# Building the scans' weights: 66 small transfers handed out between matmuls instead of in one block

## The chip, the cores and the metric

The kernel runs on one core of a Trainium2 chip. The metric is the device time of one launch in microseconds (us). TensorE (PE in the profile), VectorE (DVE), ScalarE (ACT), GpSimd (POOL) and SyncE (SP) each work through an instruction list of their own, strictly in order. They meet only through semaphores. SP and POOL also start transfers (DMA): a transfer stands in its engine's list like any other instruction, and what comes after it in the list waits until it has been issued.

## The reference: what is computed

The input x is 4 images of 96 channels and 128 x 128 pixels. Two layers follow, each added to its input. The first is a selective scan over the image in four directions:

```python
z = conv1x1(group_norm(x), in_w) + in_b             # 96 -> 192 channels
z = silu(depthwise3x3(z) + dw_b)
xs = [z row by row, z column by column, both reversed]       # 4 directions
dts, Bs, Cs = split(einsum(xs, x_proj_weight))      # 6 + 1 + 1 rows per direction
delta = softplus(einsum(dts, dt_projs_weight) + dt_projs_bias)
h[l] = exp(-exp(A_logs) * delta[l]) * h[l-1] + delta[l] * Bs[l] * xs[l]
y = sum over directions of (h * Cs + Ds * xs)
x = x + (layer_norm(y) * ln_w + ln_b) @ out_w + out_b
```

The second layer normalises x again, splits it by sign, convolves it several times (3 x 3), builds an attention between the channels whose result is used as the weights of one more 3 x 3 convolution, and mixes all of it into the output. This change concerns only the preparation of two weight tables for the scans of the first layer.

## The kernel before, in words

**Stages.** The kernel goes through: statistics of image 0; projection of image 0 (input convolution, 3 x 3 and silu in one set of matmuls); projections of images 1 to 3, with the scans woven between them; normalisations, direct maps and attention of the second layer, image by image. The first strips of image 0 are where the change lies.

**Projection (`project`).** Image 0 is worked in 16 strips of 8 rows. A strip has three groups of matmuls at L613, called q = 0, 1 and 2. The first two give channels 0 to 127 of four rows each, the third the remaining 64 channels of all eight rows. Each group fills a PSUM bank. ScalarE takes the tanh of it (L488), and VectorE multiplies it by the bank (L489); only then is the bank free. There are three such banks for everything in this stage (pool `psl`, bufs=3), given out in turn. Between q = 1 and q = 2 a small matmul (`rows_out`, L515) projects the strip before to the 48 rows that hold dts, B and C; after q = 2 twelve tiny transposing matmuls (`cols_out`, L556) follow. The input rows of the next strip are loaded by SP (L438, tile `y`), normalised by ScalarE (L456), and copied by SP into shifted positions (L464).

**Woven work.** `project` is a generator: it yields 11 times in a strip (three times in each group, and after `rows_out` and `cols_out`), so that other work can be put between. Beside the matmuls of image 0 run the statistics of images 1 and 2 (`image_stats`). Each step of them either issues a load of 96 x 512 values to a tile `xst` on POOL's list (L401) or takes `bn_stats` of such a tile on VectorE (L404). There are two tiles, so a load waits for the `bn_stats` of two loads ago. A strip holds four loads and four `bn_stats`.

**Weights of the scans (`other_weights`).** This generator makes `wdt` and `wbc`, two bf16 tables whose rows lie on the partitions in the order of the scan's input rows. It splits `dt_projs_weight` into three bf16 pieces (`split3`, ScalarE L207 and VectorE L209), then copies the pieces into place with transfers within the on-chip memory: for six row groups, three pieces, three places each, 54 transfers of 3 or 6 KB to `wdt` (L246), and for each of the six row groups two transfers of at most 0.8 KB to `wbc` (L249). All 66 are on POOL's list. After them come the output weights: VectorE scales `outw` by `lnw` (L251), TensorE makes two small products `pb` (L256) and `pw` (L263), and VectorE uses them (L259, L266).

**Order.** The top level steps these generators by hand. When two strips of image 0 are ready it takes the pair weights of the second layer (`made`, stored to `wd`), then the whole rest of `other_weights`, and only then goes on with the projection. The program is written out in this order, and every engine keeps it; from the projection of image 0 to the end of the scans, dependencies between neighbours make this explicit (`in_order`). The scans take `wdt` and `wbc` as the weights of their matmuls (L727) from the middle of image 0's projection on.

Of the kernel before, what the change touches and what calls it, by code (L numbers as in the profile page):

```python
# [62 lines left out]
def kernel(  # L63
# [138 lines left out]
    def split3(pool, src, shape):  # L202

        pieces = []
        for i in range(3):
            t = pool.tile(shape, BF16, name=f"piece{i}", tag=f"piece{i}")
            nc.scalar.copy(t, src)  # L207
            if i < 2:
                nc.vector.tensor_sub(src, src, t)  # L209
            pieces.append(t)  # L210
        return pieces

    def other_weights():

        wdt = const.tile([128, 3, NK, 128], BF16, name="wdt", tag="wdt")
        wbc = const.tile([128, 3, 2, 128], BF16, name="wbc", tag="wbc")
        outws = const.tile([C, 2, C], F32, name="outws", tag="outws")  # L220
        outbs = const.tile([C, 1], F32, name="outbs", tag="outbs")
        with (
            tc.tile_pool(name="w0", bufs=1, side="right") as w0,
            tc.tile_pool(name="ps0", bufs=1, space=PSUM, side="right") as ps0,
        ):
            wf = w0.tile([RANK, NK, 2 * C], F32, name="wf")
            nc.gpsimd.dma_start(wf, dt_wT)
            outw = w0.tile([C, 2, C], F32, name="outw")
            nc.sync.dma_start(outw, out_wT)
            one = w0.tile([3, 128], BF16, name="one")  # L230
            nc.vector.memset(one, 1.0)
            nc.vector.memset(wdt, 0.0)
            nc.vector.memset(wbc, 0.0)
            yield
            flat = "p k c -> p (k c)"
            pieces = split3(w0, wf.rearrange(flat), [RANK, NK * 2 * C])
            for row, ch, g, p, n in (
                (row, *part)
                for img, *part in PARTS
                for row in ((KI * img,) if part[1] == 1 else (0, 64))  # L240
            ):
                for w in range(3):
                    src = pieces[w].rearrange("p (k c) -> p k c", k=NK)[:, :, ch : ch + n]
                    for i in range(3):
                        at = row + w * 18 + i * RANK
                        nc.gpsimd.dma_start(wdt[at : at + RANK, g, :, p : p + n], src)  # L246
                for q in range(2):
                    at = row + 54 + q
                    nc.gpsimd.dma_start(wbc[at : at + 5 : 2, g, q, p : p + n], one[:, :n])  # L249
            for j in range(2):  # L250
                nc.vector.tensor_scalar(  # L251
                    outws[:, j], outw[:, j], lnw[:, j : j + 1], None, ALU.mult
                )
            pb = ps0.tile([C, 1], F32, name="pb")
            for j in range(2):
                nc.tensor.matmul(  # L256
                    pb, lhsT=outw[:, j], rhs=lnb[:, j : j + 1], start=(j == 0), stop=(j == 1)
                )
            nc.vector.tensor_add(outbs, pb, outb)  # L259

            pw = ps0.tile([C, C], F32, name="pw")
            for j in range(2):
                nc.tensor.matmul(  # L263
                    pw, lhsT=mean192, rhs=outws[:, j], start=(j == 0), stop=(j == 1)
                )
            nc.vector.tensor_sub(outws, outws, pw.unsqueeze(1).to_broadcast([C, 2, C]))  # L266
        yield wdt, wbc, outws, outbs
# [14 lines left out]
    def co_run(left, right, pace):  # L282


        owed = 0.0
        for cost in left:
            owed += cost * pace
            while owed > 0:
                got = next(right, 0)
                if got == 0:  # L290
                    return
                if got is None:
                    owed = 0.0
                    break
                owed -= got
# [20 lines left out]
    def traced():  # L316
        return nc.cur_bb.bb.instructions
# [21 lines left out]
    def drain(gen):  # L339
        for _ in gen:  # L340
            pass
# [48 lines left out]
    def image_stats(b, pool):  # L390

        stats = pool.tile([C, NCH, 6], F32, name="stats", tag="stats")
        mv = const.tile([C, 2], F32, name=f"stats{b}", tag=f"stats{b}")

        def run(p2, ahead, queue):
            xf = x[b].rearrange("c h w -> c (h w)")
            tiles = []
            for i in range(NCH + ahead - 1):
                if i < NCH:
                    tiles.append(p2.tile([C, CH], F32, name="xst", bufs=ahead))  # L400
                    queue.dma_start(tiles[-1], xf[:, bass.ts(i, CH)])  # L401
                yield 0.7
                if i >= ahead - 1:
                    nc.vector.bn_stats(stats[:, i - ahead + 1], tiles.pop(0))  # L404
                yield 0.7
            nc.vector.bn_aggr(mv, stats.rearrange("p c s -> p (c s)"))

        return mv, run
# [768 lines left out]
    def new_map(name):  # L1177

        m = dram.tile([C, (H + 2) * PW + 4], F32, name=name, tag=name, bufs=1)
        nc.sync.dma_start(m[:, 0:PW], zeros[:, 0:PW])  # L1180
        nc.sync.dma_start(m[:, (H + 1) * PW :], zeros[:, 0 : PW + 4])
        return m
# [13 lines left out]
    def pair_weights():  # L1196

        four, nine, taps = [], [], []  # L1200
        with tc.tile_pool(name="wq", bufs=2, side="right") as pw:
            for pair in ((aw1, aw3), (aw2, w_conv2)):
                g = pw.tile([C, 3, 3, 2, C], F32, name="g")
                for j, src in enumerate(pair):
                    v = src.rearrange("c (h w) o -> c h w o", w=3)
                    for w in range(3):

                        nc.sync.dma_start(g[:, :, w, j], v[:, :, w if j else 2 - w])
                taps.append(g)
            yield  # L1210
            for i, g in enumerate(taps):
                g = g.rearrange("p h w j o -> p h w (j o)")
                wt = pw.tile([C, 3, 4, 2 * C], F32, name="wt")
                s = pw.tile([C, 3, 2 * C], F32, name="s")
                products_weights(wt, g, s)
                for made, t in ((four, wt), (nine, g)):
                    wd = dram.tile(
                        list(t.shape), F32, name=f"wd{t.shape[2]}{i}", tag=f"wd{t.shape[2]}{i}", bufs=1
                    )
                    nc.sync.dma_start(wd, t)  # L1220
                    made.append(wd)
        yield four, nine
# [577 lines left out]
    def projections(images, weights, stats, wp, ps):  # L1800
        for b in images:
            beside = []
            for i in {0: range(1, NB - 1), 1: (NB - 1,)}.get(b, ()):
                stats[i], run = image_stats(i, wp)
                beside.append((run, nc.sync if b else nc.gpsimd))
            yield from project(
                b, weights, stats[b], beside, zb[b // 2][b % 2], xrows[b], ps
            )
            ready[b] = H // ZR
# [4 lines left out]
    with tc.tile_pool(name="wp", bufs=1, side="left") as wp:  # L1814
        stats = {}
        stats[0], run = image_stats(0, wp)
        weights = project_weights(wp)
        with tc.tile_pool(name="a0", bufs=8, side="right") as p2:
            drain(run(p2, 8, nc.sync))
        first = len(traced())  # L1820
        others = other_weights()
        for images, pace in (([0], 0.25), ([1], 0.75), ([2, 3], 1.35)):
            left = projections(images, weights, stats, wp, psl)
            if images[0] == 0:
                next(left)
                next(others)
                made = pair_weights()
                next(made)
                while ready[0] < 2:
                    next(left)  # L1830
                maps = [
                    [new_map(f"{n}{i}") for n in ("x1d", "x2d", "vd")] for i in range(2)
                ]
                four, nine = next(made)
                wdt, wbc, outws, outbs = next(others)
            co_run(left, last, pace)
            drain(left)
    istats = [ctx.enter_context(tc.tile_pool(name="istats0", bufs=1, side="left"))]
    imgs = {0: Image(0)}
    left = imgs[0].norm(yms[0][0], psl, "left")  # L1840
    co_run(left, last, 0.5)
    drain(left)
    left = direct_maps(imgs[0], psl)
# [22 lines left out]
    for b in range(NB):  # L1866
# [9 lines left out]
        left = imgs[b].attend(psl)  # L1876
# [79 lines left out]
```

## Time and profile before

| | before |
|---|---|
| median of three runs | 6881.47 us |
| lowest and highest | 6868.02 and 6881.63 us |
| span of the profiled run | 6859.9 us |
| TensorE busy | 5650.5 us (82%) |
| VectorE busy | 5060.8 us (74%) |
| POOL busy | 3478.8 us (51%) |
| mean granted TensorE clock | 0.898 |

In the profile a line such as "POOL L246 DMA_DIRECT2D wdt<-piece" is an issue on POOL's list at line 246 of the kernel; its duration is the time that the issue occupies the engine, not the time of the transfer. An idle time in brackets, such as "[5.32 <-DVE stats L404]", says how long the engine stood still just before, and which instruction's end let it go on. PEld is TensorE's loading of weights, which overlaps with its matmuls. The line numbers are those of the kernel before; in the changed kernel the same instructions lie two lines further down inside `project` and `other_weights`.

### The profile page before, as it was taken

The page shows a single profiled execution, that of the slowest core. Times are in us where ns is not written, and L with a number is a line of the kernel's source. Part 1 is how long each engine was busy: PE and PEld are TensorE (multiplying, and loading weights), DVE is VectorE, ACT ScalarE, POOL GpSimd, SP SyncE. Part 2 cuts the span into 40 slices and gives each one's busy share as a digit, 9 for nine tenths or more (in the row PEclk, how much of TensorE's full clock was granted, in tenths as well). Part 3 has the DMA queues.
Part 4 walks back from the last instruction along what each step waited for, and adds up shares of the span by engine and source line. Part 5 has one row for each costly group of instructions (what it writes and reads, how often), then busy time and mean ns, then how long its engine had stood idle before and what let it go on. Part 6 is the DMA issues. An engine that isn't in the chain of part 4 may idle for free. (4 is left out here: it accounts for less than half of the span.)

```text
span 6859.9 us, 74337 instructions
## 1 busy us (share of the span) xinstructions
PE 5650.5 (82%) x22236; PEld 2322.2 (34%) x22236; DVE 5060.8 (74%) x6916; ACT 2912.9 (42%) x3685; POOL 3478.8 (51%) x2264
## 2 busy tenths in 40 slices
PE   5889978978886539899977898887798886788987
PEld 2333323322221114444432343343343342334432
DVE  3247779979897779898458767678766778775688
ACT  1257768777875567676241122132112132121112
POOL 2236759879794339788104434334433434444641
PEclk9999989989996659999988899998899998899998
DMA  6666777866766676766767666567565667565556
GB/s 167 151 160 182 193 214 200 229 165 179 219 176 182 182 205 191 216 174 194 195 186 216 167 166 155 155 170 216 157 176 147 163 163 203 163 173 138 140 155 178
DMA packets 796460, 1227.58 MB, mean 179 GB/s; under 512 B 218750, under 2 KB 558726, under 8 KB 783580
## 3 DMA queue, kind: packets, MB, share of 16 engines
q1 hardware_dynamic: 778572, 1183.90, 63.4%
q0 software_dynamic: 16208, 38.42, 2.0%
q8 instruction: 178, 2.92, 0.2%
q14 instruction: 222, 1.82, 0.1%
q10 hardware_dynamic: 1280, 0.53, 0.0%
HBM read 858.12 MB, written 296.46 MB: 168 GB/s over the span
## 5 line engine op out<-in xcount | busy, mean ns | idle before, releaser
L613 PE MATMUL bank<-y,wp 128*128 128x512 f32 (+3 forms) x3584 | 1317.0, 626 | 94.2 <-DVE z L489 38.6
L1289 PE MATMUL bank<-t,wd 128*128 128x384 f32 (+2 forms) x4224 | 1145.5, 496 | 78.3 <-DVE s L1331 20.6
L1265 POOL TENSOR_TENSOR t<-y 128x768 f32<-128x768 f32 (+1 forms) x352 | 565.4, 1607 | 1257.2 <-PE bank L1289 391.4
L846 POOL TENSOR_TENSOR y<-y,dl 128x1024 f32<-128x1024 f32 x384 | 1051.4, 2738 | 258.6 <-DVE dl L838 228.3
L813 POOL TENSOR_TENSOR dl<-dl,u 128x1024 f32<-128x1024 f32 x384 | 1004.4, 2616 | 249.7 <-ACT dA L789 122.4
L834 DVE TENSOR_TENSOR_SCAN dA<-dA,pBC 128x512 f32<-128x512 f32 x768 | 981.4, 1278 | 30.9
L1338 ACT COPY s<-bank 128x384 f32<-128x384 f32 (+2 forms) x292 | 135.9, 465 | 1900.0 <-PE bank L1300 1837.5
L1289 PEld LDWEIGHTS bank<-t,wd 128*128 128x128 f32 (+1 forms) x4224 | 557.2, 170 | 622.0 <-issue 323.4
L727 PE MATMUL pBC<-xr,wbc 60*128 60x512 bf16 (+1 forms) x1536 | 459.9, 403 | 349.6 <-DVE dA L834 276.2
L838 DVE TENSOR_TENSOR dl<-dA,pBC 128x512 f32<-128x512 f32 x768 | 528.1, 688 | 272.3 <-PE pBC L727 199.8
L1289 PE MATMUL bank<-t,wa 128*96 128x384 f32 (+1 forms) x1408 | 561.3, 548 | 202.8 <-DVE t L1266 128.7
L613 PEld LDWEIGHTS bank<-y,wp 128*128 128x128 f32 (+3 forms) x3584 | 459.1, 169 | 764.9 <-issue 661.2
L1647 PE MATMUL bank<-y,wn 128*128 128x384 f32 (+5 forms) x2408 | 670.2, 505 | 38.4 <-ACT ring L1661 16.1
L656 ACT ACTIVATE dl<-pd,dtb 128x512 f32<-128x512 f32 x768 | 486.3, 684 | 172.0 <-PE pd L727 163.8
L817 DVE TENSOR_TENSOR pBC<-dl,pBC 128x512 f32<-128x512 f32 x768 | 527.5, 687 | 4.7 <-POOL dl L813 3.8
L1330 DVE TENSOR_TENSOR d<-s,bank 128x384 f32<-128x384 f32 (+2 forms) x292 | 155.8, 534 | 486.1 <-ACT s L1338 435.8
L789 ACT ACTIVATE dA<-dl,negA 128x1024 f32<-128x1024 f32 x384 | 420.3, 1141 | 2.3
L1647 PEld LDWEIGHTS bank<-y,wn 128*128 128x128 f32 (+3 forms) x2408 | 306.2, 167 | 335.2 <-issue 165.9
L1289 PEld LDWEIGHTS bank<-t,wa 128*96 128x96 f32 x1408 | 241.0, 184 | 507.9 <-issue 305.6
L1266 POOL TENSOR_TENSOR t<-y 128x384 f32<-128x384 f32 (+1 forms) x352 | 382.2, 1086 | 0.0
L727 PEld LDWEIGHTS <-wbc 60*128 60x128 bf16 (+1 forms) x1536 | 103.5, 96 | 781.7 <-issue 767.6
L656 ACT ACT_TABLE_LOAD x245 | 314.3, 1283 | 109.0 <-PE pd L727 102.3
(257 smaller groups left out, 7965.0 us busy)
## 6 DMA issues: line engine op xcount, KB each, us to landing
u<-zb SPq DMA_DIRECT2D x192, 1024.0 KB
yms<-y SPq DMA_DIRECT2D x96, 512.0 KB
y<-yms SPq DMA_DIRECT2D x64, 768.0 KB
xn<-xnew SPq DMA_DIRECT2D x128, 384.0 KB
y<-y SPq DMA_DIRECT2D x128, 258.2 KB
zb<-z SPq DMA_DIRECT2D x64, 512.0 KB
y<-vd SPq DMA_DIRECT2D x168, 193.8 KB
y<-in_x SPq DMA_DIRECT2D x56, 480.0 KB
```

Of the source, the lines that this page charges most:

```text
L613: nc.tensor.matmul(blocks(pz[p:e]), lhsT=ws[k][:, d, c : c + e - p], rhs=window(ys[k], at, d, n), start=(i == 0), stop=(i == len(terms) - 1),)
L656: nc.scalar.activation(dst, src, AF.Softplus, bias=bias)
L727: nc.tensor.matmul(p, lhsT=w[rows], rhs=xr[rows, at : at + CH], start=True, stop=True)
L789: nc.scalar.activation(live[m]["dA"], live[m]["dl"], AF.Exp, scale=negA[:, g % 3, k : k + 1])
L813: nc.gpsimd.tensor_mul(t, t, u_view(n))
L817: nc.vector.tensor_mul(p, live[n]["dl"][:, bass.ts(half, CH)], p)
L834: nc.vector.tensor_tensor_scan(h, h, p, init, ALU.mult, ALU.add)
L838: nc.vector.tensor_mul(live[n]["dl"][:, sl], live[n]["dA"][:, sl], live[n]["C", half])
L846: nc.gpsimd.tensor_add(v, v, t.rearrange("p (a b) -> p a b", b=W))
L1265: eng.tensor_sub(v[:, 0:2], of(y, 0), of(y, 2))
L1289: nc.tensor.matmul(pc[p:e, :n], lhsT=w[:, i, c : c + e - p], rhs=t[k][:, i, :n], start=(k == 0), stop=False,)
L1647: nc.tensor.matmul(pc[p:e, :n].rearrange("p (h w) -> p h w", w=W), lhsT=w[:, c : c + e - p], rhs=v[:, :, 0:W], start=(i == 0), stop=(i == ...
```

## The change

The loop over row groups and pieces in `other_weights` now yields ahead of each piece, 18 times in all, and the top level steps the projection of image 0 once for each of these yields:

```diff
                 for row in ((KI * img,) if part[1] == 1 else (0, 64))
             ):
                 for w in range(3):
+                    yield
                     src = pieces[w].rearrange("p (k c) -> p k c", k=NK)[:, :, ch : ch + n]
                     for i in range(3):
                         at = row + w * 18 + i * RANK
...
                 four, nine = next(made)
-                wdt, wbc, outws, outbs = next(others)
+                got = next(others)
+                while not got:
+                    next(left)
+                    got = next(others)
+                wdt, wbc, outws, outbs = got
             co_run(left, last, pace)
             drain(left)
```

So three transfers of `wdt` (after every third piece also two of `wbc`) are written out, then one step of the projection with its share of the statistics' loads, and so on. The 66 transfers stay on POOL, and their sizes stay. It is meant to let the loads of `xst` into POOL's list between the small transfers. In the built program it has two effects: seven issues of `xst` that came after the block stand earlier, one just ahead of it and six inside it (after 11, 22, 25, 39, 50 and 61 of the 66 small transfers); and the products `pb` and `pw`, with the three VectorE instructions that belong to them, come 18 steps later, among the matmuls of q = 2 in the next strip. On ScalarE and SP the order is the same.

## The prediction

> **What bounds the kernel now.** The change touches only the opening stage, the projection of image 0, so I read the busy time of each engine by stretches there first, then each engine's order of time. The columns are the stretch and its length in us, busy time (instructions) of PE, PEld, DVE, ACT, POOL, the granted PE clock, DMA share and GB/s.
>
> ```profile
> 100.00:142.00 42.00, 42.00 (x166) 16.01 (x164) 13.40 (x21) 9.36 (x14) 3.07 (x6) 1.00 0.62 152
> 142.00:163.00 21.00, 16.83 (x50) 7.10 (x46) 8.08 (x15) 3.35 (x5) 10.39 (x19) 0.92 0.74 204
> 163.00:194.00 31.00, 0.00 (x0) 0.00 (x0) 1.22 (x3) 2.40 (x3) 27.18 (x51) 0.55 0.35 80
> 203.00:264.00 61.00, 61.00 (x215) 22.62 (x213) 17.21 (x27) 13.30 (x20) 6.15 (x12) 1.00 0.62 152
> ```
>
> Around the change the stage is bound by TensorE (42.00 of 42, 61.00 of 61). From 163 to 194 us TensorE does nothing and POOL is busy 27 of 31 us. POOL's order of time there (start, duration, instruction; the idle time before it and its releaser in brackets):
>
> ```profile
> 129.82 0.51 POOL L401 DMA_DIRECT2D xst<-in_x  x1 [5.32 <-DVE stats L404]
> 143.69 1.86 POOL L246 DMA_DIRECT2D wdt<-piece  x3 [13.36 <-ACT piece L207]
> 148.38 1.62 POOL L246 DMA_DIRECT2D wdt<-piece  x3 [2.83 <-ACT piece L207]
> ...
> 165.69 4.94 POOL L246 DMA_DIRECT2D wdt<-piece  x9
> ...
> 188.78 1.08 POOL L249 DMA_DIRECT2D wbc<-one  x2
> 189.85 1.07 POOL L401 DMA_DIRECT2D xst<-in_x  x2
> ```
>
> The 66 small issues sit between two loads of xst. VectorE and TensorE over the same time:
>
> ```profile
> 151.17 0.67 DVE L489 SCALAR_TENSOR_TENSOR z<-z,bank 128x512 f32<-128x512 f32 x1
> 192.78 0.69 DVE L404 BATCH_NORM_STATS2 stats<-xst 96x6 f32<-96x512 f32 x1 [40.94 <-DMA xst<-in_x]
> 193.39 0.67 DVE L489 SCALAR_TENSOR_TENSOR z<-z,bank 128x512 f32<-128x512 f32 x1
> ```
> ```profile
> 149.31 0.95 PE L263 MATMUL pw<-outws,mean 96*96 96x96 f32 x4 [4.11 <-DVE outws L251]
> 150.05 10.93 PE L613 MATMUL bank<-y,wp 128*128 128x512 f32 x22
> 160.92 2.03 PE L515 MATMUL bank<-z,xpw 128*32 128x512 f32 x8
> 194.11 7.66 PE L613 MATMUL bank<-y,wp 128*64 128x512 f32 x28 [31.17 <-DVE z L489]
> ```
>
> So the chain is: POOL issues wdt/wbc until 189.85; the statistics of image 1 on DVE wait 40.94 us for the load behind them; the z product L489 stands behind that in DVE's order; the third PSUM bank is not freed, and PE waits 31.17 us. One more line matters, because it sets how much can come back. ScalarE:
>
> ```profile
> 149.84 0.58 ACT L488 ACTIVATE z<-bank 128x512 f32<-128x512 f32 x1
> 164.04 1.45 ACT L456 ACTIVATE y<-y,shift,rstd 96x1280 f32<-96x1280 f32 x1 [13.62 <-DMA y<-in_x]
> 165.40 0.57 ACT L488 ACTIVATE z<-bank 128x512 f32<-128x512 f32 x1
> ```
>
> ScalarE waits for the next strip's rows until 164.04 (SP issued them at 151.20 behind four stores wd of 864, 864, 648 and 648 KB). The tanh of the very bank that PE wants stands behind this.
>
> **What the Trainium skill says.** "DMA: Bandwidth & Descriptors", section "Anatomy of one DMA — SWDGE (gpsimd) path", puts a fixed cost of about 2.0 us on each such transfer, mostly completion. The trace agrees for most: 2.4 us median from wdt issue to landing, but 1.6 to 10.0 us, the long ones behind the wd stores. "Perfetto Trace Analysis", section "DMA Instruction — SWDGE (GPSIMD)", says that the shown end is that of descriptor writing, not of the data: xst shows 0.51 us and lands after 2.8. Hence I count 0.55 us of POOL per issue, not per landing. "DMA: Bandwidth & Descriptors", section "Issuing engines are not separate DMA queues", calls issue time usually small beside the transfer; here it is the whole cost, 66 times 0.55 us for 3 or 6 KB at most. "TensorE: Matmul & The Clock Gate", section "HAM oscillation — how this bites in real kernels", says idle gaps over about 3.4 us drop the PE clock; after the 31 us gap 28 half-width matmuls take 7.66 us here against 6.23 in the next strip.
>
> **The change, part by part.** The instruction streams of the two built programs differ only so: six xst issues stand between the wdt groups on POOL, and pb, pw with their three DVE products move some 1.6 strips later (PE: into the q = 2 matmuls of the next strip). Work and bytes are equal.
>
> What is lost now. A free strip takes 20.8 us (matmuls L613 start at 202.15, 222.95 and 243.75). The strip from 142.09 to 202.15 (call it A) takes 60.06, so 39.3 us are lost: 31.17 bank wait, 4.11 wait for outws, about 1.4 of pb and pw themselves, and 2.7 of slow clock (22 matmuls in 10.93 against 9.66; 7.66 against 6.23).
>
> What A costs afterwards. DVE does the pair weights and splits until 149.07 as now. Then bn_stats, and the previous strip's last z product after its tanh at 150.42, ending 151.1; the q = 1 bank of A needs it. PE ends q = 0 at 142.09 + 6.15 = 148.2, so it waits 2.9 us instead of the 4.11. Then q = 1 to 157.3 and the x projection to 159.3. For q = 2 it needs the z product of A's q = 0, whose tanh stays at 165.40 behind the late rows: product at 166.0 to 166.65, PE from 166.7. It waits 7.4 us in place of 31.17. The wd stores are not changed, so I keep 165.40; sooner by the whole 5 us or so is the outer bound. q = 2 and the transposes end at 173.5; the shifted copies of the rows, issued from 165.5, have landed by about then.
>
> Can POOL serve the loads? Each wdt or wbc is 0.549 us (44 in 24.16 us from 165.69), each xst 0.51. The xst before the block can go at about 139.1, when the 138.15 bn_stats ends. The next goes behind 11 issues, and by the eight completion semaphores taken in turn it waits for a transfer of 148.4 to land, as the tenth wdt does now: 155.1, landing by about 164 in the store traffic (the wdt beside it took 9 to 10 us), before DVE wants it at 166.7. Nine wdt and two wbc end at 165.7 as now. Then, with the built order: xst 165.7; 3 issues, xst 167.9; 14 issues, xst 176.1; 11 issues, xst 182.7; 11 issues, xst 189.2; 5 issues, xst 192.5. With 3.2 us to land they are there at 169, 171.2, 179.3, 185.9, 192.5, 195.7.
>
> What PE then wants in strip B from 173.5: its q = 0 and q = 1 run to 185.9, x projection to 187.8. DVE: bn_stats at 179.3 (product of q = 0 at 180.4 when tanh is there: no delay); bn_stats 185.9 to 186.6; residual at 188.5 as the cast comes; outws to 189.7, before pw at 190.9; bn_stats 192.5 to 193.6 after the other small products; the q = 1 product at 194.2, before PE wants its bank at 195.4. So the loads come late, yet always inside the lead of three banks, with 1.2 us to spare at the two tightest places. pb and pw cost 1.4 in B; the next strip C begins at 195.9.
>
> Sum: C begins at 222.95 now, at 195.9 then: 27.0 us. The clock is not in this: waits of 2.9 and 7.4 us should cost between 1.3 (the slowing after 4.11 us of wait at 150.05) and 2.7 (all now lost). I take 2. Gain **25 us**. For the unknown small costs: if POOL is 7 us later (as its waits on wdt landings, 6.7 us in all now, come again), 7 - 1.2 = 6 less, so 19; if the rows land 5 us sooner, 30.
>
> Does it reach the end? After this stage every engine has the same instructions in the same order, and the scan starts from strips of image 0 (first scan matmul at 309.32, waiting for xrows that those strips wrote). wdt is complete by 192.5 plus landing, over 100 us before that use. Nothing waits for a fixed time, so I carry all of it: 6881.5 - 25 = **6856 us**. The run times of before spread from 6868.02 to 6881.63, 13.6 us, so the measurement alone moves this by some 7.
>
> **Rivals.** *POOL still too late.* For: POOL is about 100% filled from 165.7 to 192.5, the margins are 1.2 us, and six loads of 192 KB join its completion semaphores. Against: 4.4 us of issues pass before a semaphore comes round, over the 1.8 to 2.8 us of most landings. With two repeats of the 6.7 us, 25 - 12 = 13 us: 6868. *The late rows were themselves an effect of the POOL block.* For: the small transfers share the DMA engines. Against: 3 MB of stores at the 204 GB/s shown is 15 us from 146.6, which is nearly 164. If so nearly all of 39.3 less pb/pw comes back: 6881.5 - 37 = 6844. *Given back later.* For: image 1 and the scan are a mixture of waits (PE bank L613 on DMA y<-y up to 17.2 us once). Against: those are relative to the same order. About 6880. *Slower.* Two such further 17.2 us waits would give 6881.5 - 25 + 34.4 = 6891; within the stage it can't be, since the last small issue moves only from 189.85 to 192.4.
>
> **How the numbers follow.** Forecast (19 to 30 us gained) 0.70; POOL too late 0.12; whole recovery 0.06; given back 0.08; slower 0.04. Over 0.2% means under 6867.7: the forecast, the whole recovery and half of the first rival, less a little for the spread, 0.81; within 0.2%: 0.15; slower 0.04. The range goes down to 6840 (whole recovery, with spread) and up to 6870 (POOL too late), leaving out about 2 in 10.
>
> **What would show it.** The wait of PE L613 on DVE z falls from 31.17 us to about 7, and ScalarE's L456 still waits about 13.6 for its rows; DVE's bn_stats has several waits of 1 to 8 us on xst, none over 12; on POOL each xst stands between wdt groups at about the times above; TensorE between 142 and 223 is idle 10 to 15 us, not 35; the first scan matmul comes at about 284, not 309. I am wrong if PE still waits over 15 us in strips A and B, if L456 comes well before 164, or if 309.32 moves by 25 and the end doesn't.

## The result and the profile after

| | before | changed |
|---|---|---|
| median of four runs | 6881.55 us | 6833.95 us |
| lowest and highest | 6868.02 and 6881.77 us | 6813.75 and 6849.30 us |
| span of the profiled run | 6859.9 us | 6836.4 us |

The ratio is 0.9934, with a 95% interval of 0.9905 to 0.9963: the changed kernel is faster, by 25 to 65 us. The median lies 22 us under my forecast of 6856 and 6 us under the low end of its range. The two profiled runs differ by 23.5 us, about what I had worked out, and the medians by 47.6 us. Why these two differences are so far apart is the main question below.

First the stage itself. The same stretches of the changed kernel (columns as before: stretch, its length, busy time of PE, PEld, DVE, ACT, POOL, granted PE clock, DMA share, GB/s):

```profile
142.00:163.00 21.00, 15.43 (x52) 5.91 (x48) 9.01 (x14) 3.35 (x5) 9.10 (x17) 0.94 0.78 219
163.00:194.00 31.00, 25.87 (x92) 9.47 (x92) 8.02 (x14) 7.07 (x11) 26.34 (x49) 0.87 0.70 158
203.00:264.00 61.00, 61.00 (x226) 22.91 (x225) 18.89 (x30) 14.04 (x21) 6.17 (x12) 1.00 0.66 161
```

From 163 to 194 us TensorE now works 25.87 of 31 us instead of none of them, while POOL is as busy as before (26.34 against 27.18): the small transfers take POOL as long as before, but the rest no longer stands still for them. TensorE in order of time:

```profile
143.18 12.29 PE L615 MATMUL bank<-y,wp 128*128 128x512 f32 x28
155.40 2.03 PE L517 MATMUL bank<-z,xpw 128*32 128x512 f32 x8
167.16 8.08 PE L615 MATMUL bank<-y,wp 128*64 128x512 f32 x28 [9.73 <-DVE z L491]
...
194.09 0.59 PE L265 MATMUL pw<-outws,mean 96*96 96x96 f32 x4 [1.06 <-DVE outws L253]
...
199.50 12.29 PE L615 MATMUL bank<-y,wp 128*128 128x512 f32 x28 [0.77 <-DVE z L491]
```

Strip A begins at 143.18 and strip C at 199.50, so the two strips take 56.3 us; before, 142.09 to 222.95, they took 80.9. The wait for a bank is 9.73 us in place of 31.17. POOL, at the places where a load of xst now stands between the small transfers:

```profile
156.44 0.54 POOL L403 DMA_DIRECT2D xst<-in_x  x1 [2.40 <-DMA wdt<-piece]
...
172.67 0.55 POOL L248 DMA_DIRECT2D wdt<-piece  x1 [1.02 <-DMA xst<-in_x]
...
180.22 0.55 POOL L403 DMA_DIRECT2D xst<-in_x  x1
...
187.28 0.55 POOL L403 DMA_DIRECT2D xst<-in_x  x1
...
195.07 0.55 POOL L403 DMA_DIRECT2D xst<-in_x  x1
```

VectorE's one wait of 40.94 us for xst has become seven between 100 and 260 us, 23.2 us in sum and 7.1 at most (the columns are sum, number and longest). ScalarE still waits for the late rows, to almost the same moment as before:

```profile
DVE stats L406 <- DMA xst<-in_x: 23.2, 7, 7.1
```
```profile
164.45 1.45 ACT L458 ACTIVATE y<-y,shift,rstd 96x1280 f32<-96x1280 f32 x1 [12.94 <-DMA y<-in_x]
165.81 0.57 ACT L490 ACTIVATE z<-bank 128x512 f32<-128x512 f32 x1
```

**Where the time goes after that.** ScalarE has the same 3685 instructions in the same order in both kernels, so the n-th of one trace can be laid beside the n-th of the other. The first column of the table is a time in the kernel before, the second how much earlier (minus) the changed kernel is at the same instruction. The third column is the same comparison of two traces of one and the same changed kernel (the second profile of it against the third, from the runs below).

| at us | changed minus before | changed minus changed |
|---|---|---|
| 140 | +1.1 | +0.7 |
| 230 | -23.5 | +1.6 |
| 700 | -22.9 | +0.7 |
| 2000 | -26.5 | +4.6 |
| 3250 | -34.5 | +6.9 |
| 4500 | -30.6 | +22.2 |
| 6750 | -26.0 | +13.5 |

The whole difference arises between 140 and 230 us, in strips A and B. To 700 us it stays as it is. Later it wanders, by up to 12 us, but so do two executions of the same program, by more. The gain is thus made where it was expected; what is added or lost after 700 us in any one pair of runs is scatter. The second profiles of the two kernels, from the runs below, are also 23.8 us apart at 230 us, but less than 3 us at 6750. So it was luck that the spans of the first two profiles differ by just the gain of the stage, and whether the gain is carried to the end must be read from the medians of many runs.

### The profile page after: what moved, and what is told of

It reads as the page before. It is cut to its first block, busy times and chain, and to the rows that moved or that the text cites. A ratio compares the mean times of both kernels' runs of the same rounds, so it can differ in the third digit from the quotient of the medians.

```text
span 6836.4 us, 74338 instructions
## 1 busy us (share of the span) xinstructions
PE 5648.3 (83%) x22236; PEld 2321.2 (34%) x22236; DVE 5053.9 (74%) x6916; ACT 2913.1 (43%) x3685; POOL 3480.8 (51%) x2264
```

## The experiments

Theory A, with which I went into the runs: the change is worth the 23.5 us seen in strips A and B, and the rest of the difference between the medians is scatter of single runs, without a cause in the kernel. Theory B: the change also raises the granted clock of all later stages, which is worth another 24 us.

**The kernel before, against itself.** No edit.

> The kernel before, against itself. Theory A (the change is worth the 23.5 us that the two traces show in strips A and B, carried to the end; what the medians differ by beyond that is scatter of single runs): ratio 1.000 within 0.2%, single runs spread over 14 us and more, each the shorter the higher its mean granted clock. Theory B (the change also makes the granted clock of all later stages better, worth another 24 us): ratio 1.000 too, but its clock lies below that of the changed kernel in nearly every run.

6867.2 us median over 22 runs (6847.9 to 6891.1), against 6861.1 over 59 runs of it (6839.4 to 6896.9): ratio 1.001 (0.9999 to 1.002). A single run of this kernel has a standard deviation of 11 us, and over the 59 runs 0.001 of mean granted clock goes with 5.3 us (correlation -0.84). The first four runs of before, 6868 to 6882, lie in the upper part of this.

**The changed kernel again.** No edit.

> The changed kernel again, more runs. Theory A: 23 to 28 us under the kernel before (ratio 0.996 to 0.9967), with single runs scattered by 14 to 35 us along the granted clock. Theory B: 45 to 50 us under it (ratio 0.993), with a mean clock higher by 0.002 or more.

6832.4 us median over 22 runs, ratio 0.9963 (0.9951 to 0.9974): 25.4 us (18 to 34). A to C takes 56.9 us. Its mean clock is 0.9007 against 0.8989, close to the 0.002 that B named, but this isn't a better clock later. In the first pair of profiles the granted clock from 100 us to the same place in strip C is 0.87 over 130 us in the kernel before and 0.95 over 107 us in the changed one. That is 0.13 x 130 - 0.05 x 107 = 11.6 us of full clock, 0.0017 of 6860; after it both have 0.90. The idle stretch that the change removed, with its 0.55, was itself a slow part of the average.

**The pause put back elsewhere.**

```diff
         first = len(traced())
+        with tc.tile_pool(name="pause", bufs=1, side="right") as pz:
+            hold = pz.tile([128, 2048], F32, name="hold")
+            for _ in range(13):
+                nc.vector.memset(hold, 0.0)
```

> The changed kernel with 13 VectorE memsets of 128 x 2048 (a pause of about 25 us) between the statistics and the projection of image 0, where every engine waits for VectorE; nothing is left out. Theory A: the pause costs what the change gave, so the time is that of the kernel before within 0.2% (6878 to 6885 us). Theory B, by which it is the mix of work and rest in strips A and B that improves the clock later: still 20 to 25 us under the kernel before.

6864.9 us median over 22 runs, ratio 1.0006 (0.9996 to 1.0016). A pause of some 27 us (ScalarE's instructions at 100 us start 27.0 us later than in the kernel before) takes away the whole gain; at 230 us the two kernels are 3.5 us apart. Its mean clock is 0.9004, about that of the changed kernel, without any of its gain. Theory B falls, by these runs and by the 25.4 us of the section before: time taken out of strips A and B is worth about that time at the end, within some 8 us.

**The stores of the pair weights given out too.** The generator of the pair weights yields ahead of each store; the top level takes one every fourth step.

```diff
+                    yield
                     nc.sync.dma_start(wd, t)
                     made.append(wd)
...
-                four, nine = next(made)
                 got = next(others)
+                pairs = next(made)
+                n = 0
                 while not got:
                     next(left)
                     got = next(others)
+                    n += 1
+                    if n % 4 == 0 and not pairs:
+                        pairs = next(made)
                 wdt, wbc, outws, outbs = got
+                four, nine = pairs
```

> The changed kernel, with the four stores of the pair weights (3 MB, wd) also given out one by one, every fourth step, so that the next strip's rows no longer stand behind 3 MB of stores. By my step on the late rows (L456 waits until 164 because of the stores): ScalarE's wait of 12.9 us for the rows falls to under 5, TensorE's 9.7 us wait in strip A goes, the clock drop after it (8.08 us in place of 6.23) goes, and the time falls by a further 8 to 12 us against the changed kernel. Rival (the rows are late because of the small transfers on POOL, or VectorE's split work sets the wait): ScalarE still waits until 160 or later, gain under 3 us.

6822.3 us median over 6 runs, ratio 0.995 (0.9932 to 0.9967). ScalarE and then TensorE of this kernel:

```profile
152.27 1.45 ACT L458 ACTIVATE y<-y,shift,rstd 96x1280 f32<-96x1280 f32 x1 [3.91 <-DMA y<-in_x]
```
```profile
157.06 6.23 PE L615 MATMUL bank<-y,wp 128*64 128x512 f32 x28
163.22 0.52 PE L558 MATMUL bank<-pick,rp 64*128 64x32 bf16 x12
164.56 12.29 PE L615 MATMUL bank<-y,wp 128*128 128x512 f32 x28 [0.83 <-DVE z L491]
...
184.99 0.95 PE L265 MATMUL pw<-outws,mean 96*96 96x96 f32 x4 [3.02 <-DVE outws L253]
185.88 6.12 PE L615 MATMUL bank<-y,wp 128*64 128x512 f32 x16
```

The rows come at 152.27 instead of 164.45 (SP issues their load at 147.48, ahead of all four stores, instead of at 152.49 behind them), strip A has no bank wait, and its q = 2 matmuls take 6.23 us instead of 8.08. So the stores did cause the late rows, as the prediction had it. But A to C takes 49.7 us (142.87 to 192.53), only 6.7 less than in the changed kernel: with TensorE earlier, the loads behind the small transfers are now too late in strip B. VectorE waits up to 9.5 us for xst, pw waits 3.02 us through it, and the 16 matmuls after that wait take 6.12 us where the changed kernel's take 3.66. The medians differ by 10.0 us, inside the expected 8 to 12, but the intervals of the two ratios overlap, so this number decides nothing beyond the trace.

**Six steps in place of 18.** One yield for each row group, so 11 small transfers at a time.

```diff
-                for w in range(3):
-                    yield
+                yield
+                for w in range(3):
```

> The changed kernel with 6 yields in place of 18: 9 small wdt and 2 wbc transfers at a time (6 us of POOL) between steps of 2 us of matmuls. Theory A (POOL's order and the loads' lateness against the lead of three banks): the 66 issues must go out within about 12 us of matmul time, so only one or two loads fit in between, VectorE waits 12 us at a time for xst, and TensorE waits 15 to 25 us in all in strips A and B; from the start of strip A to that of strip C 62 to 72 us (56.3 in the changed kernel, 80.9 before); time 8 to 18 us under the kernel before. Rival (any break in the block is enough): as the changed kernel, 56 to 58 us.

6864.6 us median over 12 runs, ratio 0.9995 (0.9982 to 1.0007): no gain that can be told from none, where 8 to 18 us were expected. TensorE:

```profile
170.38 0.95 PE L265 MATMUL pw<-outws,mean 96*96 96x96 f32 x4 [9.80 <-DVE outws L253]
171.26 7.92 PE L615 MATMUL bank<-y,wp 128*64 128x512 f32 x28
183.47 0.79 PE L558 MATMUL bank<-pick,rp 64*128 64x32 bf16 x12 [4.29 <-DVE rp L531]
201.10 14.42 PE L615 MATMUL bank<-y,wp 128*128 128x512 f32 x28 [16.83 <-DVE z L491]
...
224.02 11.43 PE L615 MATMUL bank<-y,wp 128*128 128x512 f32 x26
```

A to C is 78.1 us (145.90 to 224.02), more than the 62 to 72 that I expected. The direction was right (any break in the block is not enough), the size was not: one load got in between, at 177.23, after 33 of the 66 small transfers, and the next ones not before 196.00, after the other 33, so VectorE waited 8.99 and 16.44 us for xst; and TensorE's waits add to 30.9 us against 35.3 before. What counts is how many transfers stand between two loads, not that there is a break.

**36 steps.** A second `yield` ahead of each piece.

> The changed kernel with two yields ahead of each piece, so that the 66 transfers spread over 36 steps (3.3 strips). Theory A: VectorE's waits for xst shrink below 3 us each, the small waits of TensorE in strip B (1.06 and 0.77 us) go, strip A's wait of 9 to 10 us for its bank stays as the late rows set it; A to C 53.5 to 55.5 us; time 1 to 3 us under the changed kernel, which these runs can't tell from it. Rival (the loads' lateness also sets the wait in A): A's wait falls under 6 us.

6848.3 us median over 6 runs, ratio 0.9973 (0.9956 to 0.999), which can't be told from the changed kernel. In the trace A to C is 53.4 us:

```profile
168.73 7.61 PE L616 MATMUL bank<-y,wp 128*64 128x512 f32 x28 [10.34 <-DVE z L492]
...
197.52 12.29 PE L616 MATMUL bank<-y,wp 128*128 128x512 f32 x28
```

The waits in strip B are gone and VectorE waits only once for xst (2.2 us), yet the 10.34 us in strip A stay: they are not the loads' doing. Some 1.1 us of the difference is pb and pw, which fall past strip C here.

**The small transfers left out.** The two `dma_start` lines of `wdt` and `wbc` are taken out, all else stays.

> The changed kernel without the 66 small transfers: the two weight tables stay zero, so the scans work on zero weights; all else is there. It bounds what any handling of these transfers can bring. Theory A: A to C 53 to 55 us, with strip A's wait of 9 to 10 us still there, and ScalarE still waiting until about 164 for its rows: all but 1 to 3 us was already had by the change. Rival (the late rows come from the small transfers in the shared DMA engines): the wait falls under 5 us, A to C about 46.

6839.0 us in one run. A to C is 54.6 us (143.37 to 197.95), with

```profile
167.43 8.33 PE L615 MATMUL bank<-y,wp 128*64 128x512 f32 x28 [9.81 <-DVE z L491]
```
```profile
164.73 1.45 ACT L458 ACTIVATE y<-y,shift,rstd 96x1280 f32<-96x1280 f32 x1 [13.03 <-DMA y<-in_x]
```

so without any of these transfers the rows are just as late. Of what the 66 transfers cost, 80.9 - 54.6 = 26.3 us in the traces, the change has got back all but 1.7.

**Only the output weights later.** The 66 transfers in one block, then 18 yields, then pb, pw and their VectorE work.

> Only the second effect of the change: the 66 transfers in one block as before, the products pb and pw 18 steps later. Theory A: the bank wait of about 31 us in strip A stays (35 in fact, as the wait of 4.1 us for outws goes but POOL's block ends at the same time), A to C 80 to 83 us, nothing gained. Rival (moving pb and pw off strip A brings 4 us of the gain): A to C 76 to 77 us.

6871.9 us in one run. A to C is 81.7 us (143.42 to 225.15):

```profile
195.24 7.73 PE L616 MATMUL bank<-y,wp 128*64 128x512 f32 x28 [37.57 <-DVE z L492]
```

The 4.11 us that TensorE no longer waits for outws come back in the bank wait, which is 37.57 us now, as POOL's block ends when it did. In the trace, the change's second effect alone gives nothing.

**The changed kernel on another chip, and both limits removed.** The first is the changed kernel; the second has the spread stores and the second `yield` together.

> The changed kernel once more, beside the next run. Theory A: 0.9957 to 0.9972 of the kernel before (19 to 29 us), wherever the level of the kernel before lies on this chip. Theory B: a gain of 45 us or more as the first four runs of each showed.

> The changed kernel with the stores of the pair weights spread and the small transfers over 36 steps. Theory A (two separate limits: rows behind stores in strip A, loads behind small transfers in strip B): both waits go, A to C 42 to 45 us (41.6 is two free strips), TensorE never idle over 2 us from strip A to C, 11 to 14 us under the changed kernel, ratio to the kernel before about 0.9945. Rival (with the stores spread, another transfer or VectorE's pair-weight work takes the place): A to C 47 us or more, as in the run with the stores spread alone.

The changed kernel: 6837.1 us median over 7 runs, 0.9971 (0.9956 to 0.9986), 20 us (10 to 30); A to C 56.0 us. With both limits removed: 6820.2 us over 5 runs, 0.9929 (0.9916 to 0.9942), 49 us (40 to 58) under the kernel before. Its TensorE:

```profile
145.30 12.29 PE L616 MATMUL bank<-y,wp 128*128 128x512 f32 x28
157.52 2.03 PE L518 MATMUL bank<-z,xpw 128*32 128x512 f32 x8
159.49 6.23 PE L616 MATMUL bank<-y,wp 128*64 128x512 f32 x28
165.65 0.52 PE L559 MATMUL bank<-pick,rp 64*128 64x32 bf16 x12
167.00 12.29 PE L616 MATMUL bank<-y,wp 128*128 128x512 f32 x28 [0.83 <-DVE z L492]
...
187.80 12.29 PE L616 MATMUL bank<-y,wp 128*128 128x512 f32 x28
```

A to C is 42.5 us, 0.9 over two free strips of 20.8: almost nothing is left to win here. The trace accounts for 80.9 - 42.5 = 38.4 us, or about 37 once pb and pw, which have moved past strip C, are counted; the ratio says 40 to 58, a little more than the 0.9945 (38 us) that was expected. The part beyond the trace is not explained by anything in these strips and isn't larger than the wandering in the table above.

## Why the prediction was wrong

**The chain and the gain in the stage: right.** Each step stands beside its measurement; strip A began 1.1 us later in the profiled run of the changed kernel, so times after A's start are compared.

| step | predicted | measured |
|---|---|---|
| q = 2 of A, after A's start | 24.6 us | 24.0 us |
| waits in A | 2.9 and 7.4 us | 9.73 us, one wait |
| loss by the clock | 2 us | 8.08 - 6.23 = 1.9 us |
| A to C (with that loss) | 55.8 us | 56.3 us |
| gain from A to C | 25 us | 80.86 - 56.32 = 24.5 us |
| first scan matmul | about 284 us | 285.9 us |

Two terms in it were off and hardly moved the sum, which was luck. The wait of 2.9 us ahead of q = 1 of strip A is not there: 28 matmuls run through in 12.29 us from 143.18, so that group did not wait for the last product of the strip before, which VectorE began only at 151.54, and TensorE reached the second wait earlier. And POOL was slower than counted: its issues of xst come at the forecast times (plus the 1.1 us) up to 169.47, but then 3.0, 3.5, 4.8 and 4.7 us late, because it waited for landings (1.02 us in the line above, others of 0.45 to 1.14). I had taken 3.2 us for a load to land; in this stretch it is 4.6 in the median and up to 8.4. The 1.2 us to spare were used up, which shows as waits of 1.06 and 0.77 us. So POOL was late in the way of the first rival, "*POOL still too late*", but it cost 1.8 us and not its 6 or 12.

**"*The late rows were themselves an effect of the POOL block*": wrong as a rival.** With the transfers left out the rows come no sooner (164.73); with the stores spread they come 12 us sooner. **"*Given back later*" and "*Slower*": wrong.** The medians of many runs, 25.4 us (18 to 34) under the kernel before, and the pause show the gain carried to the end, within some 8 us.

**The step that failed** is the last of the sum: "so I carry all of it: 6881.5 - 25 = **6856 us**", with "the measurement alone moves this by some 7". The gain in it was right, the level it was taken from was not. Over the 110 later runs of the kernel before (22 of them as a kernel of its own), on three chips, the median is 6863.9 us, 17.6 under the 6881.5 that three runs had given; 5 of the 110 reach 6881. The 29 later runs of the changed kernel have 6836.0, close to the 6833.95 of the first four. 6863.9 - 25 would have been 6839, and the range of 6840 to 6870, moved down by the same 17.6, would have held both medians of the changed kernel. The direct comparisons, 25.4 us (18 to 34) and 20 us (10 to 30), agree with the 25. So the mis-sized term is the starting level, by 17.6 us, and the range was too narrow for it: with 11 us of spread in a single run (14 in the changed kernel's 22), medians of three or four runs each leave the difference uncertain by some 10 us, an estimate from 1.25 x 11 / sqrt(3.5) for each side, against the 7 that I allowed for the whole. The profile page already showed a span of 6859.9 us for the same kernel, and the time of that run, 6861.66 us, is 19.8 under the median; I saw the two levels and did not ask which of them was the unusual one.

What stays open is why the first runs of the kernel before were so long: three of the four lie within 0.3 us of each other, at 6881.5 to 6881.8. Scatter like that of the later runs, to which theory A put it down, hardly explains this: with 5 of 110 at 6881 or more, three or more of four would come about 4 times in 10,000, an estimate from 4 x (5/110)^3. The medians of the three chips, 6861.1, 6870.8 and 6867.1 us, show that the level moves from one set of runs to another, but none of them reaches 6881. The clocks of those first runs and the chip they ran on are not known here.

## What to carry to other kernels

A queue that issues transfers in order is an engine like the others: 66 transfers of a few KB held TensorE for 26 us, by way of one load behind them, one VectorE instruction behind that, and a bank. Break up such a block by how many issues the waiting load can stand ahead of it (with three banks of lead, up to 14 issues of 0.55 us between two loads did little harm, 33 took nearly the whole gain away), and look at once for what is ready to take the wait's place: here stores on another queue, worth some 12.5 us more in the trace together with a wider spread. And before subtracting a gain from a level, know how far the level itself moves: a forecast of half a per cent needs more than three runs under it.

## What the runs showed of the hardware that was not expected

Loads of 192 KB took longer to land in the changed kernel: between 140 and 210 us 4.6 us in the median and 8.4 at most, against 2.7 and 3.1 in the kernel before, whose loads in that stretch all came after the block. The small transfers are not the reason, since with them left out it is 4.9 in the median and 10.0 at most. What the reason is was not tested; the mean DMA share of that stretch is 0.72 in the changed kernel, 0.67 with the transfers left out and 0.50 before.

And the mean granted clock of a run, which is 0.001 lower with 5.3 us more of its time, can rise without any gain: the kernel with the pause has 0.9004, the kernel before 0.8989, at the same time within 0.16%. It has lost the idle stretch at 0.55, as the changed kernel has, and its own pause, in which TensorE does next to nothing, stands in the record at 1.00 (50 to 80 us).
